# A four-layer cross-attention network: the first layer's attention tail with GpSimd and VectorE in written order

## The chip, the cores and the metric

The kernel runs on one core of a Trainium2 chip. The metric is the time of one execution on the device in microseconds (us). Three runs of the kernel before gave 1819.81, 1826.41 and 1832.21 us; the median is 1826.41. A core has five engines that run beside each other, each working through its own list of instructions in order: TensorE (PE in the profile; its weight loads are listed apart as PEld), VectorE (DVE), ScalarE (ACT), GpSimd (POOL) and SyncE (SP, which here only issues transfers). They wait for each other through semaphores.

## What is computed

Four layers in a row update 2048 tokens of width 256. Each layer adds a cross-attention to a context of 1601 rows and then a feed-forward part:

```python
x = x + _L0_xattn_ref(_layernorm(x, axis=-1), ctx_1024, ...)
x = x + _L0_ffn_ref(_layernorm(x, axis=-1), L0_ffn_gate_w, L0_ffn_experts)
x = x + _L1_xattn_ref(_layernorm(x, axis=-1), ctx_1024, mask_BxSxS2_ik0, L1_xattn_Wq, L1_xattn_Wk, L1_xattn_Wv)
x = x + _L1_ffn_ref(_layernorm(x, axis=-1), L1_ffn_fast_b, L1_ffn_w_fc, L1_ffn_w_proj, L1_ffn_u, L1_ffn_v, L1_ffn_gate)
...
```

The part that matters here is `_L1_xattn_ref`, an attention with one head of width 256 in which keys whose mask is 0 get a score of -1e10, and `_L1_ffn_ref`, whose two weight matrices are rounded to -1, 0 and 1 times a scale of each row. Layers are counted from 0 in the reference, so what the change's short name calls the first layer is L1.

## The kernel before, in words

The tokens are kept on chip as 16 tiles of 128 rows (`self.x`), in four chunks of four tiles. `network` (L2154) runs the layers. Everything from L1 on lies in a conditional block (L2164), chosen by a number that `experts0` works out.

**How the order of the work is set.** The kernel is written in a framework that records the instructions in the order of the source and then schedules them: for each engine it chooses an order by priorities and by its own estimate of when operands are ready. `tc.manual_schedule(engines=...)` excepts the engines it names, which keep the order of the source until the surrounding `ExitStack` closes. `experts0` (L552), `ffn1` (L1387), `ffn2` (L1522) and `attention3_tail` (L1947) name all four computing engines (`IN_ORDER`, L18), `attention0` names TensorE alone (L441). `attention1_tail`, which the change touches, names none.

**`attention1_tail` (L1101).** Only the last 400 of 1601 keys (L29, `K0`, `NTAIL`) are open. They are worked on as four key tiles of 100. L1123 to L1147 transpose the three weight matrices (L225, copied by ScalarE at L234) and make keys and values (L1134, L1143). Then each chunk of tokens goes through two parts.

The generator `prepare(c)` (L1149) makes a chunk ready:

- `fetch` (L789) has GpSimd gather the rows that the experts of layer 0 owe to the four tiles (L794, an indirect transfer each), and VectorE adds them (L799).
- `norm_steps` (L144): VectorE takes the statistics of each tile (L151, L152), GpSimd makes 1/sqrt of the variance (`rstd`, L156 and L157), VectorE normalises (`xn`, L171), TensorE transposes (L185), ScalarE copies out of the accumulator bank (`xnT`, L189).
- TensorE projects to queries (L1158); ScalarE copies them (L1162), VectorE copies them again as bf16 (L1163).
- For each of the four tiles TensorE makes bf16 scores (L1169) and adds the mask (L1173), and VectorE takes their maximum (L1174). The four maxima are transposed to a row (L247) and cast to `shift` by VectorE (L248).

The loop (L1183) then makes the scores of chunk c (L1192), takes the shift off in the same accumulation (L1195), has ScalarE take exponentials (L1196), and for each tile sums the values (L1202) and has VectorE divide and add (L1209 and L1210). The value sums use accumulator banks with tag "a", of which there are two, and all of `self.pm()` (transposes, projections, maxima) uses banks with tag "m", also two (L92). Between these steps the source calls `step(nxt, ...)`, which takes the next chunk's `prepare` a step further, and `step(beside, 2)` (L1207).

**`beside`** is `ffn1_weights` (L1253), the preparation of the next part's weights, a generator as well. Its VectorE work in this stage: the mean absolute values of the rows of `w_fc` (L1280 to L1283, L1289), eight ternary groups (two instructions, L1222 and L1223, then the scaling of `u`, L1293), the low-rank part (L1312 to L1332), the same for `w_pr` (L1280 to L1283 and four pairs of L1222 and L1223), and at the end the first input of `ffn1` (`inputs(0)`, L1366). TensorE transposes the ternary matrices (L1232, L1245), ScalarE copies them (L1235, L1249). GpSimd clears two tiles (L1304 and L1321). SyncE loads `w_fc`, `w_pr` and small inputs at the start, and later the weights of the following layers into the same three buffers (`wraw`, L63), each as soon as its buffer is free.

After this stage `ffn1` (L1379) runs; its first matmul is at L1396.

Of the kernel before, what the change touches and what calls it, by code (L numbers as in the profile page):

```python
# [40 lines left out]
def drain(gen):  # L41
    if gen is not None:
        for _ in gen:
            pass
# [10 lines left out]
class Net:  # L55
# [1045 lines left out]
    def attention1_tail(self, pre, mask, raw, due, beside=None):  # L1101

        tc, nc = self.tc, self.nc
        with ExitStack() as s:
# [44 lines left out]
            def prepare(c, made):  # L1149
                self.fetch(rows, range(c * TPC, (c + 1) * TPC), *due)  # L1150
                xnT = self.norm(c)
                yield
                q = qp.tile([P, 2, CH], F32, name="q")
                qb = qp.tile([P, 2, CH], BF16, name="qb")
                for o in range(2):
                    ps = self.pm()
                    for kc in range(2):
                        nc.tensor.matmul(  # L1158
                            ps, lhsT=wT["Wq"][:, kc, o * P : (o + 1) * P], rhs=xnT[:, kc, :],
                            start=kc == 0, stop=kc == 1,  # L1160
                        )
                    nc.scalar.copy(q[:, o, :], ps)  # L1162
                    nc.vector.tensor_copy(qb[:, o, :], ps)  # L1163
                yield
                m = self.small.tile([P, TPC], F32, name="m")
                for i in range(TPC):
                    ps = self.pm()
                    for kc in range(2):
                        nc.tensor.matmul(  # L1169
                            ps[:, :NTAIL], lhsT=qb[:, kc, i * P : (i + 1) * P], rhs=kb[:, kc, :],  # L1170
                            start=kc == 0, stop=False,
                        )
                    nc.tensor.matmul(ps[:, :NTAIL], lhsT=one, rhs=away, start=False, stop=True)  # L1173
                    nc.vector.tensor_reduce(m[:, i : i + 1], ps[:, :NTAIL], AX.X, ALU.max)  # L1174
                    yield
                shift = shifts[c % 2]
                self.row_from_columns(lambda i: m[:, i : i + 1], shift[0:1])
                made.append((q, shift))

            made = []  # L1180
            drain(prepare(0, made))
            self.ready = 0
# [1047 lines left out]
```

## Time and profile before

| what | value |
|---|---|
| median of three runs | 1826.41 us (1819.81 to 1832.21) |
| profiled execution, its own time | 1826.28 us |
| its span, from the first to the last instruction | 1824.2 us |
| mean granted TensorE clock | 0.976 |
| TensorE busy | 1699.6 us (93%) |
| VectorE, ScalarE, GpSimd busy | 909.8, 728.5, 690.8 us |
| first TensorE instruction of the stage (L225) | 863.3 us |
| first TensorE instruction of `ffn1` (L1396) | 978.15 us |

Times in the profile count from the start of the span; 2.1 us of the execution lie outside it. "Busy" counts the time in which an engine runs an instruction. In the list of groups a row is one line of the kernel on one engine: the operation, its output and inputs, how often it ran, its busy time and the mean duration of one in ns, and then the engine's idle time before these instructions and what ended it. In the list of waits a row says who waited for whom, for how long in all, how often, and the longest. In the table by stretches each row is a stretch of the span, its length, and then the busy time of each engine with the number of instructions, the granted TensorE clock (1.00 is full speed), the busy share of the transfer engines and what they moved. In the timeline a row is one instruction or a run of equal ones: start, duration, engine, line, operation, and in brackets the idle time before it and what ended it. A TensorE instruction on 32-bit data shows as two records, except for transposes.

VectorE and GpSimd reach the stage before TensorE does: VectorE's first instruction in it (L1114) starts at 831.80, GpSimd's (L1130) at 831.88, while TensorE is still in the last products of `experts0` (L557) until 863. In the order before, VectorE's first normalisation (L171) waits 24.1 us for GpSimd's `rstd`, which stands behind the clearing at L1304, and that starts at 867.66.

### The profile page before, as it was taken

The numbers are of one execution on the slowest core, as the hardware profiler recorded it, in microseconds if no ns is written. First come the engines' busy times: TensorE is split into PE (matmuls) and PEld (weight loads), VectorE is DVE, ScalarE is ACT, GpSimd is POOL, SyncE is SP. The second block draws the span as 40 slices with busy tenths as digits, with TensorE's granted clock in tenths as the row PEclk, the third lists the DMA queues.
The fourth block names the chain that finished last, engine by engine and source line by source line (L and its number), as shares of the span: only waits on it lengthen the run. The fifth ranks groups of instructions, "written<-read, shape, count | busy, mean of one in ns | idle before, by whom it ended". The sixth has DMA issues, their size and how long they took to land.

```text
span 1824.2 us, 21267 instructions
## 1 busy us (share of the span) xinstructions
PE 1699.6 (93%) x8102; PEld 848.0 (46%) x8102; DVE 909.8 (50%) x1737; ACT 728.5 (40%) x963; POOL 690.8 (38%) x477
## 2 busy tenths in 40 slices
PE   6879999999999998999999999999988789999898
PEld 3323334333333334444457863664576622332687
DVE  4664565555664543662844643422045567786300
ACT  3554443453443442223234522111135456666222
POOL 2047886876887683002202730100026400211210
PEclk9889999999999998999999999999989889999999
DMA  8870000000000000454300010000000001010651
GB/s 271 280 229 1 1 1 1 1 1 1 1 1 1 1 0 12 163 220 173 111 13 1 1 32 1 1 1 0 0 1 1 13 13 21 17 22 13 221 184 39
DMA packets 52461, 94.11 MB, mean 52 GB/s; under 512 B 10093, under 2 KB 37374, under 8 KB 51454
## 3 DMA queue, kind: packets, MB, share of 16 engines
q1 hardware_dynamic: 49776, 88.92, 14.8%
q0 software_dynamic: 768, 2.10, 0.4%
q10 hardware_dynamic: 1806, 1.64, 0.3%
q8 instruction: 66, 1.08, 0.2%
q14 instruction: 45, 0.37, 0.1%
HBM read 69.30 MB, written 19.01 MB: 48 GB/s over the span
## 4 chain that ended last, share of the span: by engine, by line
PE 72%; DVE 12%; ACT 5%; DMA 4%; POOL 3%; issue 3%; SPq 0%; ACTq 0%; DVEq 0%; POOLq 0%
PE pa L472 8%; PE psc L460 6%; PE pa L557 6%; PE psc L1058 5%; PE pa L1078 5%; PE psc L1980 4%; DVE mp L385 4%; PE pa L2143 3%; PE psc L2132 3%; DVE ri L422 3%; PE pa L1449 2%; PE psc L458 2%; ACT p L1987 2%; PE pm L380 2%; PE pm L431 2%
## 5 line engine op out<-in xcount | busy, mean ns | idle before, releaser
L481 POOL TENSOR_TENSOR sp<-sp,p 128x1024 f32<-128x1024 f32 (+1 forms) x176 | 418.5, 2378 | 57.7 <-ACT p L465 47.0
L385 DVE TENSOR_REDUCE mp<-pm 128x1 f32<-128x512 f32 x384 | 242.8, 680 | 159.7 <-PE pm L380 159.0
L465 ACT ACTIVATE p<-psc 128x1024 f32<-128x1024 f32 (+1 forms) x208 | 212.9, 1024 | 260.5 <-PE psc L460 166.9
L460 PE MATMUL psc<-qT,kT 64*128 64x512 f32 (+1 forms) x832 | 221.6, 594 | 0.0
L472 PE MATMUL pa<-p,v 128*64 128x512 f32 (+1 forms) x832 | 202.3, 608 | 0.0
L1987 ACT ACTIVATE p<-psc 100x1024 f32<-100x1024 f32 x128 | 124.4, 1021 | 62.7 <-PE psc L1980 54.7
L1965 DVE TENSOR_REDUCE ms<-psc 128x2 bf16<-128x800 f32 x128 | 124.2, 988 | 46.0 <-PE psc L1961 43.4
L380 PE MATMUL pm<-kb,qb 64*128 64x512 bf16 x384 | 100.5, 389 | 27.5 <-DVE mp L385 26.0
L557 PE MATMUL pa<-w_e,xe 128*128 128x512 f32 x256 | 118.7, 614 | 0.0
L472 PEld LDWEIGHTS pa<-p,v 128*64 128x64 f32 (+1 forms) x832 | 50.9, 137 | 129.8 <-issue 126.8
L1058 PE MATMUL psc<-q,kT 128*128 128x512 f32 (+1 forms) x208 | 102.2, 610 | 0.0
L171 DVE TENSOR_SCALAR xn<-x,mv,rstd 128x256 f32<-128x256 f32 x128 | 58.2, 512 | 87.7 <-PE pm L185 52.2
L156 POOL TENSOR_SCALAR rstd<-mv 128x4 f32<-128x4 f32 x32 | 9.8, 308 | 228.6 <-DVE mv L152 185.2
L1078 PE MATMUL pa<-v,p 128*128 128x257 f32 (+1 forms) x416 | 95.3, 382 | 0.0
L460 PEld LDWEIGHTS psc<-qT,kT 64*128 64x128 f32 (+1 forms) x832 | 86.0, 185 | 19.5 <-issue 6.3
L1980 PE MATMUL psc<-q,kT 32*100 32x512 f32 x512 | 82.0, 653 | 13.2 <-ACT p L1987 11.5
L458 PE MATMUL psc<-sh,negz 64*128 64x512 bf16 (+1 forms) x416 | 87.7, 384 | 2.1 <-ACT sh L407 2.0
L1030 DVE TENSOR_REDUCE mp<-pm 128x1 f32<-128x512 f32 x64 | 34.4, 571 | 102.5 <-PE pm L1025 102.2
L1078 PEld LDWEIGHTS pa<-v,p 128*128 128x128 f32 (+1 forms) x416 | 77.5, 190 | 11.8 <-issue 0.2
L567 ACT COPY y<-pa 128x512 f32<-128x512 f32 x64 | 37.6, 587 | 96.6 <-PE pa L557 94.3
L557 PEld LDWEIGHTS pa<-w_e,xe 128*128 128x128 f32 x256 | 48.0, 194 | 55.6 <-issue 52.3
L479 POOL TENSOR_TENSOR sp<-p,p 128x1024 f32<-128x1024 f32 x16 | 37.7, 2354 | 89.4 <-ACT p L465 89.4
(376 smaller groups left out, 2730.2 us busy)
## 6 DMA issues: line engine op xcount, KB each, us to landing
table<-y SPq DMA_DIRECT2D x32, 512.0 KB, 3.2
w<-in_L_ffn_w_dram SPq DMA_DIRECT2D x16, 1024.0 KB, 6.2
head<-in_mask_BxSxS_ik_dram SPq DMA_DIRECT2D x16, 600.5 KB, 4.0
head<-in_mask_1x1xSxS_ik_dram SPq DMA_DIRECT2D x16, 600.5 KB, 4.0
bc<-turned SPq DMA_DIRECT2D x7, 1024.0 KB, 7.0
tail<-in_mask_BxSxS_ik_dram SPq DMA_DIRECT2D x16, 200.0 KB, 4.1
tail<-in_mask_1x1xSxS_ik_dram SPq DMA_DIRECT2D x16, 200.0 KB, 3.6
x<-in_x_dram SPq DMA_DIRECT2D x16, 128.0 KB, 4.0
```

Source lines behind the costliest of these rows:

```text
L380: nc.tensor.matmul(pair[j][:, :wd], lhsT=qb[h, i * P : (i + 1) * P], rhs=kb[h, hp, k0 : k0 + wd], start=True, stop=True,)
L385: nc.vector.tensor_reduce(mp[:, i, j, n : n + 1], pair[j][:, :wd], AX.X, ALU.max)
L460: nc.tensor.matmul(sc[:r, j, :], lhsT=kT[h, hp, kt * P : kt * P + r], rhs=q[h, :], start=False, stop=True,)
L465: nc.scalar.activation(p[:r], sc[:r], AF.Exp, scale=DH**-0.5)
L472: nc.tensor.matmul(acc[h, :], lhsT=v[:r, kt, hp * P + h.start : hp * P + h.stop], rhs=p[:r, j, :], start=kt == 0, stop=kt == NKT - 1,)
L481: nc.gpsimd.tensor_tensor(sums[:r], sums[:r], p[:r], ALU.add)
L557: nc.tensor.matmul(ps, lhsT=xnT[t // TPC][:, kc, (t % TPC) * P : (t % TPC + 1) * P], rhs=ew[kc][:, 2 * h : 2 * h + 2, :], start=kc == 0, s ...
L1058: nc.tensor.matmul(sc[:r, j, :], lhsT=kT[:, kc, ks], rhs=q[:, kc, :], start=kc == 0, stop=False)
L1078: nc.tensor.matmul(acc[:, : D + 1], lhsT=p[:r, kt, i * P : (i + 1) * P], rhs=v[:r, kt, :], start=kt == 0, stop=kt == NKT - 1,)
L1965: nc.vector.tensor_reduce(ms[u % 2][:, i, 64 * k + DH : 64 * k + 64 : 32], ps[:, :, :NTAIL], AX.X, ALU.max)
L1980: nc.tensor.matmul(sc[j // 2][:TR, j % 2, :], lhsT=kT[h, g, kt * TR : (kt + 1) * TR], rhs=q[u][h, :], start=True, stop=True,)
L1987: nc.scalar.activation(p[:TR], sc[k][:TR], AF.Exp, scale=DH**-0.5)
```

## The change

One line is added in `attention1_tail`, ahead of the first chunk's `prepare`:

```diff
@@ -1177,6 +1177,7 @@
                 self.row_from_columns(lambda i: m[:, i : i + 1], shift[0:1])
                 made.append((q, shift))
 
+            s.enter_context(tc.manual_schedule(engines={mybir.EngineType.Pool, mybir.EngineType.DVE}))
             made = []
             drain(prepare(0, made))
             self.ready = 0
```

From there to the end of the function GpSimd and VectorE keep the order of the source; that takes in the steps of `prepare` and of `beside` that are called from it. TensorE and ScalarE are scheduled as before, around the two fixed lists, and their order differs too. No instruction is added or taken away. The order in which SyncE issues its transfers is the same. Lines after L1179 have a number higher by one in the changed kernel.

What the changed lists look like: on GpSimd the row fetches of chunk 1 come after the `rstd` of chunk 0, those of chunk 2 after that of chunk 1, and those of chunk 3 after that of chunk 2 and after both clearings (L1304, L1321), where before twelve fetches stood ahead of the first `rstd`. VectorE's list, with the lines of before, goes:

```
chunk 0: L799 x4, (L151 L152) x4, L171 x4, L1163 x2, L1174 x4, L248
chunk 1: L799 x4, (L151 L152) x4, L171 x4, L1163 x2, L1174 x3
w_fc:    L1280 to L1289, (L1222 L1223 L1293) x4
         L1209 L1210, L1174, (L1222 L1223 L1293) x4, L1209 L1210, L248, (L1209 L1210) x2
chunk 2: L799 x4, (L151 L152) x4, L171 x4, L1163 x2, L1174 x3
         L1312 x2, L1209 L1210, L1174, L1314 to L1332, L1209 L1210, L248
w_pr:    L1280 to L1283, (L1222 L1223) x4, (L1209 L1210) x2
chunk 3: L799 x4, (L151 L152) x4, L171 x4, L1163 x2, L1174 x3
         L1209 L1210, L1174, then the statistics of ffn1's first inputs
...
```

## The prediction

> **What bounds the kernel now.** I read the page first, for the busiest engine and the chain of work that ended last:
>
> ```profile
> span 1824.2 us, 21267 instructions
> PE 1699.6 (93%) x8102; PEld 848.0 (46%) x8102; DVE 909.8 (50%) x1737; ACT 728.5 (40%) x963; POOL 690.8 (38%) x477
> ...
> PE 72%; DVE 12%; ACT 5%; DMA 4%; POOL 3%; issue 3%; SPq 0%; ACTq 0%; DVEq 0%; POOLq 0%
> ```
>
> TensorE carries the chain, so a wait costs time only where TensorE stands still for it. Next the busy time by stretch, for the stage that the change touches: its TensorE work runs from 863.3 us (the first L225) to 978.15 us (the first L1396 of ffn1).
>
> ```profile
> core 0: us, PE busy (x) PEld busy (x) DVE busy (x) ACT busy (x) POOL busy (x), PEclk, DMA share, GB/s
> 863.30:978.15 114.85, 112.31 (x438) 58.99 (x436) 66.09 (x183) 35.34 (x58) 13.20 (x18) 1.00 0.17 54
> 863.30:886.96 23.66, 21.12 (x82) 10.52 (x80) 15.02 (x43) 8.42 (x20) 7.93 (x10) 1.00 0.58 182
> 886.96:908.00 21.04, 21.04 (x89) 11.59 (x89) 19.21 (x54) 5.50 (x9) 1.48 (x2) 1.00 0.16 51
> 908.00:936.00 28.00, 28.00 (x108) 13.57 (x107) 17.20 (x51) 10.30 (x15) 2.53 (x4) 1.00 0.09 29
> 936.00:960.00 24.00, 24.00 (x98) 12.85 (x97) 8.93 (x25) 6.74 (x11) 1.26 (x2) 1.00 0.00 1
> 960.00:978.15 18.15, 18.15 (x67) 10.46 (x65) 5.72 (x14) 4.38 (x6) 0.00 (x0) 1.00 0.00 0
> ```
>
> TensorE idles 114.85 - 112.31 = 2.5 us, all before 886.96. That caps any gain. VectorE is nearly full from 887 to 908 (19.21 of 21.04) yet holds nobody up. The waits of TensorE in the stage, and GpSimd's longest in front of work:
>
> ```profile
> PE pm L1169 <- DVE qb L1163: 0.9, 2, 0.5
> PE pm L225 <- ACT WkT L234: 0.8, 1, 0.8
> PE psc L1195 <- DVE shift L248: 0.3, 1, 0.3
> ...
> POOL b L1304 <- PE pm L1134: 19.7, 1, 19.7
> ```
>
> **The change, part by part.** No instruction is added or removed; order alone changes. VectorE now runs the layer strictly as written: a chunk's row additions, its statistics, its normalisation, its maxima, and the weight preparation (`beside`) in one lump where each step is called. GpSimd likewise. TensorE and ScalarE are still scheduled, and their order is new too. I laid the new orders side by side with durations from this trace. VectorE's lumps:
>
> ```profile
> L1280 DVE TENSOR_REDUCE sc<-w_fc 128x8 f32<-128x2048 f32 x1 | 2.3, 2289 | 0.0
> L1222 DVE TENSOR_SCALAR lo<-w_fc,nhalf 128x256 bf16<-128x256 f32 x8 | 2.7, 339 | 0.0
> L1223 DVE SCALAR_TENSOR_TENSOR tfc<-w_fc,half,lo 128x256 bf16<-128x256 f32 x8 | 3.8, 472 | 0.0
> ...
> L1280 DVE TENSOR_REDUCE sc<-w_pr 128x2 f32<-128x2048 f32 x1 | 2.2, 2240 | 0.0
> L1222 DVE TENSOR_SCALAR lo<-w_pr,nhalf 128x512 bf16<-128x512 f32 x4 | 1.9, 472 | 0.0
> L1223 DVE SCALAR_TENSOR_TENSOR tpr<-w_pr,half,lo 128x512 bf16<-128x512 f32 x4 | 3.0, 738 | 0.0
> ```
>
> In the timeline a dependent VectorE instruction starts about 0.05 us after its producer's end, an independent one about 0.08 before. So one w_fc group (L1222, L1223, then L1293) takes 0.93 us and one w_pr pair 1.32. On TensorE, start to start, a score instruction L1192 takes 0.945 us (two records), L1195 0.34, a value instruction L1202 0.485, a tile's maxima (L1169 twice, L1173) 0.61. The line numbers are those of before. PSUM tag "a" has two buffers: the third L1202 group of a chunk needs the first freed by L1210, the fourth the second.
>
> *1, hand-over from chunk 0.* Removed: the 0.9 and 0.3 us above (score instructions now stand in front of the waiting L1169). Added: shift 0.8 (0.11 hand-over, 0.67 cast, 0.05), because chunk 1's transposes no longer stand there. Then VectorE, from the shift on: 0.6, four row additions 1.56, four statistics pairs 2.2, GpSimd's rstd 1.5 (L156 and L157 with hand-overs), first xn 0.45: 6.3 us; TensorE: 0.6 of the wait, four L1192 and four L1195 (5.1): 5.7. It waits 0.5, and 0.2 for the next xn. Net +0.3.
>
> *2, w_fc lump.* It sits between the third maximum of chunk 1 and L1210 of chunk 0's first tile. VectorE from the third maximum's matmul: 0.6 for the maximum, L1280 2.2, L1281 to L1289 0.6, four groups 3.75, L1209 and L1210 0.7: 7.9 us. TensorE meanwhile: one L1202 0.5, the last maxima 0.6, three L247 0.3, four L1192 3.8: 5.2. Wait 2.7. Then the L1232 transposes: one of the two "m" banks is held for the shift, whose cast waits behind the second half of the lump, so twice they wait for ScalarE's copy (0.11 + 0.59 + 0.05), and once 0.9 for the last ternary group. In all 2.7 + 2.4 = +5.1.
>
> *3, chunk 2's rows.* As in 1, VectorE needs 0.7 (L1209, L1210) and 5.7 (additions to first xn); TensorE has 6.0 us of filler. Wait 0.5 and 0.2: +0.7.
>
> *4, w_pr lump.* First 0.5 for L1210 behind L1314 to L1332. Then shift 0.6, L1280 2.2, small ones 0.6, four pairs 5.3, L1209 and L1210 0.6: 9.3 us, against 1.9 + 5.1 + 0.5 (L1202, scores, L1245) = 7.6 on TensorE. Wait 1.6. Together +2.1.
>
> *5, chunk 3's rows.* VectorE: L1209 and L1210 0.6, then 5.8 to the first xn: 6.4. TensorE has only eight L1202, 3.9: wait 2.4. Then L1158 waits for the copy of xnT without filler, 0.7. +3.1.
>
> *6, ffn1's statistics.* Eight pairs (3.4 us), spread over idle VectorE time before, now stand ahead of an L1210: 0.5 + 3.4 + 0.8 = 4.7 against 2.8 of TensorE work. +1.9.
>
> Sum: 0.3 + 5.1 + 0.7 + 2.1 + 3.1 + 1.9 = 13.2 us.
>
> *Clock.* Here is what a light stretch does elsewhere in this trace, in three neighbouring stretches and the transposes in the middle one:
>
> ```profile
> 1407.98:1411.40 3.42, 2.41 (x18) 2.15 (x18) 3.42 (x13) 2.88 (x3) 2.15 (x2) 1.00 0.00 0
> 1411.40:1414.81 3.41, 1.39 (x8) 1.00 (x9) 3.41 (x3) 0.47 (x1) 2.04 (x1) 0.98 0.00 0
> 1414.81:1418.22 3.41, 3.41 (x10) 2.67 (x9) 3.09 (x12) 0.70 (x3) 0.00 (x0) 0.52 0.00 0
> ...
> 1413.65 1.09 PE L185 MATMUL pm<-ident,xn 128*128 128x128 f32 x6 [2.02 <-DVE xn L171]
> ```
>
> TensorE busy 1.39 of 3.41 us was followed by 3.4 us at half clock: 1.7 us lost. Gaps 2 and 5 can each make such a stretch, depending on where the stretches fall: 0 to 3.4; I take one, +1.7. The Trainium skill, "TensorE: Matmul & The Clock Gate", section "HAM oscillation — how this bites in real kernels", warns only of idle gaps over about 3.4 us. By that rule gaps of 2.7 and 2.4 are free and the sum stays 13.2 (1839.5); the row above, halved after a gap of 2.02, contradicts it.
>
> *Moved on queues, costed at nothing.* GpSimd's two memsets (L1304, L1321) and the fetches of rows 12 to 15 move behind chunk 2's rstd, from about 868 to 922; first use about 940 and 951, the fetch lands within 6.1 us. Fetches 8 to 11 wait for chunk 1's rstd (889), used at 916. On SP the load of w_dn waits for the last w_fc group (891 to about 912), the next layer's three weights for the last w_pr pair (910 to about 951); first uses are 1064 and 1057.8. If such a cover were gone, the lateness would be paid whole. Chunk 0's rstd leaves its place behind L1304: its xn is ready about 25 us sooner, but TensorE did not wait for it.
>
> Total 13.2 + 1.7 = 14.9 us. After the stage ffn1 is again bound by TensorE, so nothing returns it. The profiled execution took 1826.28 us, the median is 1826.41: 1826.3 + 14.9 = 1841 us.
>
> **The rivals.** *A. The new TensorE order covers VectorE's lumps.* For: at hand-overs 1 and 3 it does, to 0.7 us. Against: both lumps outlast the filler by 1.6 to 2.7. If only 1 stood: 1826.6 us. *B. GpSimd freed from L1304 gains.* For: 19.7 us of wait vanish. Against: the cap, 2.5 us: 1823.8. *C. The half clock follows every gap, and it is slower by over 1%.* Places: 2 (twice), 4, 5, 6. With four at 1.7 it is 13.2 + 6.8: 1846.3. It decides from three on (18.3 us). For: the rows above. Against: gaps of 1.6 and 1.9 leave TensorE over 1.5 busy in 3.4, more than 1.39, and at 2.41 the clock stayed 1.00.
>
> **How the numbers follow.** Forecast 0.55 (its own range 1836 to 1844), A and its shades 0.10, B 0.04, C or lumps dearer than summed 0.31. About 1% (18.3 us) is what a measurement of this kernel can tell from no change; the forecast, A and most of B lie within it. Faster 0.02, same 0.67, slower 0.31. The range goes down to 1832 (half of the waits gone) and up to 1852 (20 us of C, and 6 us, since the runs of before spread by as much above the median).
>
> **What would show it.** Right: TensorE idle near 16 us between the first L225 and ffn1, in waits of L1202 for L1210 and of L185 for L171, the longest about 2.7 us, beside the lumps; a slice at half clock at one of them; the rest of the span unchanged. Wrong: no idle time beside the lumps (A), half clock three times or more (C), or a wait for a row fetch or a memset, whose cover I would have misjudged.

## The result, and the profile after

The changed kernel took 1849.54 us in the median (1842.94 to 1855.18), the kernel before 1828.36 beside it: ratio 1.0113 [1.0085, 1.0141]. Taken a second time (e5 below) it was 1848.57 against 1826.42, 1.0120 [1.0091, 1.0150]. That is 21 to 22 us slower, inside the range given (1832 to 1852), above the forecast of 1841 and its own range (1836 to 1844). The prediction gave 0.67 to a change of up to about 1% and 0.31 to a larger loss; the measured ratio lies a little past 1%, but its interval holds 1% too, so it does not decide between the two.

The page of the changed kernel (profiled execution 1852.77 us), first its span and busy times, then the shares of the chain of work that ended last:

```profile
span 1850.8 us, 21249 instructions
PE 1716.3 (93%) x8090; PEld 857.5 (46%) x8102; DVE 917.8 (50%) x1737; ACT 727.7 (39%) x963; POOL 689.7 (37%) x477
...
PE 71%; DVE 14%; ACT 5%; DMA 4%; POOL 3%; issue 3%; SPq 1%; ACTq 0%; DVEq 0%; POOLq 0%
```

TensorE still carries the chain, but VectorE has 14% of it in place of 12, and TensorE's own busy time grew by 16.7 us though it executes the same instructions. Where that happened shows in the busy time by stretch of the changed kernel; the first row is the stage from its first L225 to the first L225 of the next layer, the others stretches within it (columns as in the prediction; the lines of the changed kernel behind L1179 are one higher):

```profile
864.90:1081.00 216.10, 199.53 (x887) 130.07 (x886) 118.90 (x275) 77.84 (x118) 65.42 (x58) 0.95 0.10 31
...
908.00:936.00 28.00, 22.47 (x77) 12.90 (x76) 16.39 (x48) 6.54 (x10) 6.38 (x8) 0.82 0.18 56
936.00:960.00 24.00, 22.17 (x82) 10.29 (x82) 18.40 (x39) 8.33 (x10) 0.00 (x0) 0.97 0.06 18
960.00:978.15 18.15, 16.72 (x64) 8.75 (x63) 8.60 (x25) 3.79 (x7) 1.28 (x2) 0.95 0.08 20
978.15:1000.00 21.85, 20.10 (x69) 11.52 (x68) 10.66 (x35) 4.38 (x6) 2.52 (x4) 0.84 0.00 1
```

In the kernel before the same stage ran from 863.3 to 1057.8, all at full clock:

```profile
863.30:1057.80 194.50, 188.57 (x886) 125.25 (x885) 113.42 (x274) 77.80 (x118) 63.08 (x56) 1.00 0.10 32
```

That is 194.5 us, of which TensorE was busy 188.57. So the stage has grown by 21.6 us, and that splits in two: idle time 5.93 -> 16.57, +10.6, and busy time 188.57 -> 199.53, +11.0. The rest of the 26.6 us by which the profiled span grew (1.6 us ahead of the stage, 3.4 behind it) lies in stages that the change does not touch. Those vary by some us from profile to profile: two profiles of the changed kernel have 769.9 and 767.0 us behind the stage, while the stage itself took 216.1 and 216.0. The waits of TensorE in the changed kernel's stage (total, times, longest):

```profile
PE pa L1203 <- DVE x L1211: 4.8, 3, 2.8
PE pm L185 <- DVE xn L171: 2.7, 3, 1.3
PE pa L1203 <- DVE ri L1210: 1.5, 1, 1.5
PE pm L1233 <- DVE shift L248: 0.8, 1, 0.8
...
PE psc L1196 <- DVE shift L248: 0.8, 1, 0.8
PE pm L1233 <- ACT wfT L1236: 0.7, 1, 0.7
```

These are the waits of the prediction's steps: the value matmuls (L1202 before) wait for the division that stands behind a weight lump, the transposes wait for the normalised rows, and the waits for qb (L1169 before) are gone. What the waits do to the clock shows in the changed kernel's busy time by stretches of 3.41 us (in each trace the half-clock stretches all begin on one grid of this length, and the stretches are cut along it), a light one and its successor each time:

```profile
907.30:910.70 3.40, 0.76 (x2) 0.00 (x0) 3.26 (x13) 0.00 (x0) 0.00 (x0) 1.00 0.00 0
910.70:914.10 3.40, 3.29 (x8) 2.64 (x9) 3.29 (x11) 0.00 (x0) 0.00 (x0) 0.50 0.00 0
...
955.00:958.45 3.45, 1.96 (x11) 0.79 (x10) 3.27 (x8) 1.99 (x3) 0.00 (x0) 1.00 0.01 2
958.45:961.85 3.40, 3.40 (x10) 2.67 (x9) 3.30 (x12) 0.00 (x0) 0.00 (x0) 0.50 0.81 230
...
978.95:982.35 3.40, 1.67 (x10) 1.23 (x8) 3.08 (x14) 0.00 (x0) 1.69 (x4) 1.00 0.00 0
982.35:985.80 3.45, 3.45 (x10) 1.74 (x9) 1.47 (x5) 0.00 (x0) 0.84 (x1) 0.50 0.02 5
```

TensorE is busy 0.76, 1.96 and 1.67 us of 3.4, and what follows runs at half clock for 10.2, 3.4 and 6.8 us: six stretches, 20.5 us, where the kernel before had none. Half of six full stretches is 10.2 us, which is nearly all of the 11.0 by which the busy time grew.

### The profile page after: what moved, and what is told of

It reads as the page before. It is cut to its first block, busy times and chain, and to the rows that moved or that the text cites. A ratio compares the mean times of both kernels' runs of the same rounds, so it can differ in the third digit from the quotient of the medians.

```text
span 1850.8 us, 21249 instructions
## 1 busy us (share of the span) xinstructions
PE 1716.3 (93%) x8090; PEld 857.5 (46%) x8102; DVE 917.8 (50%) x1737; ACT 727.7 (39%) x963; POOL 689.7 (37%) x477
## 3 DMA queue, kind: packets, MB, share of 16 engines
q10 hardware_dynamic: 1806, 1.64, 0.3%
## 4 chain that ended last, share of the span: by engine, by line
PE 71%; DVE 14%; ACT 5%; DMA 4%; POOL 3%; issue 3%; SPq 1%; ACTq 0%; DVEq 0%; POOLq 0%
PE pa L472 8%; PE psc L460 6%; PE pa L557 6%; PE psc L1058 5%; PE pa L1078 5%; PE psc L1981 4%; DVE mp L385 4%; PE psc L2133 3%; PE pa L2144 3%; DVE ri L422 3%; PE pa L1450 2%; PE psc L458 2%; PE pm L380 2%; PE pa L1998 2%; PE pm L431 2%
## 5 line engine op out<-in xcount | busy, mean ns | idle before, releaser
L1981 PE MATMUL psc<-q,kT 32*100 32x512 f32 x512 | 83.0, 659 | 13.2 <-ACT p L1988 11.5
```

Source lines behind the costliest of these rows:

```text
L1981: nc.tensor.matmul(sc[j // 2][:TR, j % 2, :], lhsT=kT[h, g, kt * TR : (kt + 1) * TR], rhs=q[u][h, :], start=True, stop=True,)
```

## The experiments

Theory V: VectorE's work, put in lumps by the source's order, makes TensorE wait, and the waits make the half clock; each is about half of the loss. Rivals: G, it is GpSimd's order; O, it is the fixed order as such or TensorE's new order, whatever VectorE has to do; L, the half clock in this stage is luck of the moment. The measure throughout is the stage, from its first L225 to the next layer's, in the profiled execution; beside it the ratio of the whole time to the kernel before, measured beside it each time (its medians were 1826.4 to 1833.6 us).

| kernel | stage us | TensorE idle | busy | half-clock stretches | ratio |
|---|---|---|---|---|---|
| before | 194.5 | 5.9 | 188.6 | 0 | |
| changed | 216.1 | 16.6 | 199.5 | 6 | 1.0113 [1.0085, 1.0141] |
| e5, changed again | 216.0 | 16.6 | 199.4 | 6 | 1.0120 [1.0091, 1.0150] |
| e1, GpSimd alone | 202.9 | 12.2 | 190.7 | 1 | 1.0050 [1.0034, 1.0066] |
| e2, VectorE alone | 219.8 | 20.0 | 199.8 | 6 | 1.0137 [1.0113, 1.0161] |
| e3, casts, scheduled | 201.6 | 10.9 | 190.7 | 2 | 1.0046 [1.0030, 1.0062] |
| e4, casts, in order | 209.3 | 14.1 | 195.2 | 4 | 1.0063 [1.0039, 1.0087] |
| e6, division first | 208.8 | 15.1 | 193.7 | 2 | 1.0091 [1.0070, 1.0112] |
| e7, gaps filled | 212.2 | 9.8 | 202.4 | 2 | 1.0086 [1.0066, 1.0106] |
| e10, rows ahead | 211.1 | 14.9 | 196.2 | 5 | 1.0071 [1.0052, 1.0090] |

**e1, GpSimd alone in order; e2, VectorE alone.**

```diff
-s.enter_context(tc.manual_schedule(engines={Pool, DVE}))
+s.enter_context(tc.manual_schedule(engines={Pool}))      # e1
+s.enter_context(tc.manual_schedule(engines={DVE}))       # e2
```

> Only GpSimd is kept in the source's order; VectorE is scheduled as before. Measure: TensorE's time from the stage's first L225 to the next layer's first L225, 194.5 us in the kernel before and 216.1 in the changed one; PE waits of the stage about 2.5 and 12 us. Theory V (VectorE's lumps make the waits, and the waits make the half-clock stretches): the lumps are gone, so 194 to 196 us, no wait of a value matmul for its division and no half-clock stretch in the stage; whole time 1824 to 1830. Rival G (GpSimd's order carries the loss, its rstd or its fetches coming late): 205 us or more, with waits of L185 behind it. Rival L (the half clock in the stage is luck of the phase, not of the waits): half-clock stretches here as well, 10 us of them, without waits.

> Only VectorE is kept in the source's order; GpSimd is scheduled as before. Theory V: as slow as the changed kernel, 212 to 219 us from the stage's first L225 to the next layer's (before 194.5, changed 216.1), the same waits of L1203 (2 to 3 us at each weight lump), perhaps with a longer wait for the normalised rows of chunk 1 (2.1 us in place of 0.6), since GpSimd's rstd stands behind the memset that waits for its memory. Whole time 1842 to 1852. Rival G: 195 to 200 us, near the kernel before.

e2 came as theory V has it: 219.8 us, the same waits of L1203 (2.75, 0.33, 1.49, 1.73), and longer ones for xn (3.13 and 2.47), six half-clock stretches. VectorE's order is enough for the whole loss. e1 missed: expected 194 to 196, it took 202.9 and the whole kernel 0.5% longer. The cause shows in its timeline (start, length, engine, line, in brackets the idle time before and its releaser), for VectorE, GpSimd and TensorE:

```profile
873.64 2.29 DVE L1281 TENSOR_REDUCE sc<-w_fc 128x8 f32<-128x2048 f32 x1 [30.40 <-PE pm L1143]
...
876.11 0.23 POOL L156 TENSOR_SCALAR rstd<-mv 128x4 f32<-128x4 f32 x1 [37.14 <-DVE mv L152]
...
878.06 2.31 PE L185 MATMUL pm<-ident,xn 128*128 128x128 f32 x8 [3.72 <-DVE xn L171]
```

VectorE, scheduled anew since GpSimd's order had changed, has the reduction of w_fc in front of the last aggregate of chunk 0's statistics (L152, 875.85). The reduction does not start until 873.64; the releaser named does not touch w_fc, and in e3 ScalarE's first cast of w_fc waited for that weight's load until 872.84, so the load is the likely cause. Behind it hang GpSimd's rstd, and, in order behind that, the fetches of chunk 1 (877.7 to 882.7; in the kernel before they had been issued by 843). TensorE waits 3.72 for xn and 2.38 more for qb. In the changed kernel, with VectorE in order too, that rstd runs at 844.93. So GpSimd's order alone does cost, 8.4 us of the stage, but by a mechanism that the two together do not have.

**e3, e4, the ternary instructions taken off VectorE.** The same edit to the kernel before (e3) and the changed one (e4):

```diff
-            self.ternary(tp, tfc[:, o, :], wfc[:, o, :], half[:, o : o + 1], nhalf[:, o : o + 1])
+            nc.scalar.copy(tfc[:, o, :], wfc[:, o, :])
...
-            self.ternary(tp, tpr[:, o, :], wpr[:, o, :], half[:, o : o + 1], nhalf[:, o : o + 1])
+            nc.scalar.copy(tpr[:, o, :], wpr[:, o, :])
```

> The kernel before, with the ternary weights of ffn1 left out: in place of the two VectorE instructions of each piece ScalarE casts the weight to bf16 (so the weights used are not the ternary ones). It is the base for the next kernel. Theory V and its rivals alike: 194 to 198 us from the stage's first L225 to the next layer's, since VectorE's lumps were off the path before; waits of TensorE 3 to 5 us.

> The changed kernel with the same edit: ternary instructions left out, ScalarE casts instead (so the weights used are not the ternary ones). The in-order engines stay in order; only the two big lumps on VectorE shrink, by 4 x 0.8 us each half of w_fc and 4.8 us for w_pr. Theory V: the waits at the lumps vanish, the change then costs 1 to 5 us beside the scheduled kernel with the same edit, in place of 21.6: 196 to 201 us from the stage's first L225 to the next layer's, one wait of 1.5 to 2 us left (at ffn1's statistics), 0 to 3.4 us at half clock. Rival O (the order as such costs, that is TensorE's own new order, or the rows' additions and statistics at the hand-overs): 10 us or more remain. Rival L (half clock by luck): the waits go, but 10 us of half-clock loss stay.

Both stages are longer than expected by a wait that the edit itself made in both: L1143 stands 4.6 us behind ScalarE, whose first cast waits for the load of w_fc, and two half-clock stretches follow. Between the two, the order costs 7.7 us in place of 21.6: idle +3.2, busy +4.5, two half-clock stretches more. The whole times, 1839.76 against 1838.10, differ by less: in these two profiles the parts outside the stage took 5.4 us less in e4, so the 7.7 rests on the stage alone. The waits at both lumps are gone, as theory V says; left are 1.25 for the rows of chunk 2 and 1.73 at ffn1's statistics, each followed by half clock. The sum of 1 to 5 us was too low, again by the clock. Rival O (10 us or more) is not borne out, but about a third of the loss stays without the ternary lumps.

**e5, e6, e7: the same waits again, the wait moved, the wait filled.**

```diff
                     step(nxt, 1)
-                    step(beside, 2)
                     ri = self.small.tile([P, 1], F32, name="ri1")
                     nc.vector.reciprocal(ri, acc[:, D : D + 1])
                     nc.vector.scalar_tensor_tensor(x, acc[:, :D], ri, x, ALU.mult, ALU.add)
+                    step(beside, 2)
```

is e6; e7 adds to the changed kernel, ahead of tile 2 of chunks 0 and 2, and once more behind the first scores of chunk 2:

```diff
+                    for n in {(0, 2): (2, 2), (2, 2): (2, 2)}.get((c, i), ()):
+                        fill = self.pm()
+                        for _ in range(n):
+                            nc.tensor.matmul(fill, lhsT=self.ident, rhs=q[:, 0, :], start=True, stop=True)
                     acc = self.pa()
```

> The changed kernel itself once more, as the base for the next two on the same chip. Theory V (VectorE's lumps make TensorE wait about 12 us in the stage, and the waits make the half-clock stretches): 214 to 220 us from the stage's first L225 to the next layer's, half-clock stretches again near the waits of L1203, 17 to 21 us of them; whole time 1845 to 1853. Rival L (the half clock in the stage was luck): the waits again, but the half-clock stretches elsewhere or gone, 203 to 208 us.

> The changed kernel with a tile's division and update (L1210, L1211) written ahead of the weight preparation's step instead of behind it. Theory V: the three waits of L1203 for x and ri (2.75, 1.48, 1.74 us) vanish, since what TensorE waited for no longer stands behind a lump; the lump now delays the next chunk's maxima, shift and rows instead, so that part returns as waits of L185 for xn (up to 3.7 us) and of L247 for m (1.3). 3 to 7 us less than the changed kernel from the stage's first L225 to the next layer's: 209 to 213. Rival O (the lumps delay in whatever place): no change beyond 2 us.

> The changed kernel with eleven matmuls that nothing uses (128x512 f32, 0.47 us each, 5.2 us in all) put on TensorE ahead of the three waits of L1203 that were 2.75, 1.48 and 1.74 us long: four, three and four of them. The work waited for is the same, so it comes no sooner. If a wait cost only its own length, the time stays as it is (5.0 us of the added work lies in the waits, 0.2 outside). Theory V with the clock as second cost: the stretches of 3.41 us around these three waits stay busy above 2 us, so that the half clock behind them goes: three to five of six half-clock stretches, 1.7 us each, so 5 to 9 us less than the changed kernel, 207 to 212 us from the stage's first L225 to the next layer's, though TensorE has more to do. Rival L (half clock by luck): as slow as the changed kernel or 5 us slower.

e5: the six half-clock stretches lie in the same places, 10.2, 3.4 and 6.8 us, behind the same waits. Rival L, as chance from run to run, falls here. But the stage also began at the same place of the 3.41 us grid in both profiles (2.0 and 2.1 us into a stretch), so e5 does not show what another place would do; e2 does (see e8). e6: the waits of L1203 are gone, and what was expected in their place is there, in this line of its timeline:

```profile
954.66 1.74 PE L185 MATMUL pm<-ident,xn 128*128 128x128 f32 x8 [3.64 <-DVE xn L171]
```

Idle time fell by only 1.5 us; busy time fell by 5.8, since two half-clock stretches are left of six. 208.8 us, where 209 to 213 were expected.

e7 is the clearest. Its eleven matmuls are 22 records that start 0.43 us apart; from the first record of each group to the next instruction they take 9.7 us in all, nearly twice what the expectation's text says. The stage by stretch, and TensorE's wait of L1203 (L1211 in this kernel):

```profile
861.30:1073.50 212.20, 202.44 (x909) 130.78 (x908) 118.95 (x275) 77.87 (x118) 65.52 (x58) 0.98 0.10 32
```

```profile
PE pa L1211 <- DVE x L1219: 0.3, 1, 0.3
```

TensorE has 9.7 us more to do, waits 6.8 less, and has two half-clock stretches in place of six, which is worth 6.8: 9.7 - 6.8 - 6.8 = -3.9 us, and -3.9 is what the stage shows. That is less than the 5 to 9 us expected, since more work was added than planned. The whole kernel took 1842.50 against 1848.57 in the median of six runs each (1839.28 to 1844.61 and 1839.37 to 1855.20). A wait's length and its clock are separate costs, and the second can be taken away while the first stays.

**e8, gaps of graded length, in the kernel before.** In ffn1, ahead of every second slot:

```diff
+            def gap(size):
+                first = self.pm(BF16)
+                tc.nc.tensor.transpose(first[:, :P], self.identb, self.identb)
+                tc.nc.vector.tensor_copy(slow[:, :P], first[:, :P])
+                w = wfT.rearrange("p k f -> p (k f)")[:, :size].bitcast(F32)
+                tc.nc.vector.tensor_tensor(slow[:, :size], w, w, ALU.add)
+                then = self.pm(BF16)
+                tc.nc.tensor.transpose(then[:, :P], slow[:, :P], self.identb)
```

> The kernel before, with seven gaps of graded length put into ffn1, where TensorE is busy without a break: a transpose, a VectorE sum over 256 to 2048 columns behind it, and a transpose that needs the sum. Gaps of about 0.8, 1.1, 1.3, 1.6, 2.0, 2.4 and 2.7 us, 8 us apart or more. It measures what a gap costs beyond its own length. By the reading behind the prediction (half clock once TensorE is busy 1.4 us or less in a stretch of 3.41): only the gaps of 2.0 and more that fall within one stretch, so one to three half-clock stretches. By the changed kernel's trace (half clock also behind stretches with 1.68 and 1.93 us): gaps from 1.6 us up, two to four. Rival L (no relation): half clock behind short gaps as often as behind long ones.

Other VectorE work stood ahead of the gaps' sums, so the gaps came out at 6.37, 1.64, 5.63, 1.96, 5.90, 2.17 and 5.54 us. The whole took 1868.85 us in its one run, the stage 232.5 in place of 194.5: 29.2 of gaps, and nine half-clock stretches. The four over 5 us are each followed by two. The three short ones tell more; here those of 1.64 and 1.96 with the stretch behind them:

```profile
1005.06:1008.48 3.42, 1.78 (x17) 1.61 (x16) 2.60 (x4) 1.42 (x3) 1.89 (x1) 1.00 0.00 0
1008.48:1011.89 3.41, 3.41 (x21) 2.95 (x21) 2.93 (x9) 1.50 (x3) 1.28 (x2) 1.00 0.00 0
...
1035.78:1039.19 3.41, 1.45 (x14) 1.27 (x12) 2.58 (x4) 1.34 (x3) 1.89 (x1) 0.97 0.01 2
1039.19:1042.61 3.42, 3.42 (x10) 2.71 (x10) 3.42 (x16) 0.35 (x1) 0.42 (x1) 0.53 0.00 0
```

The gap of 1.96 lies in one stretch, leaves 1.45 busy, and the next runs at half clock; the gap of 1.64 (1.78 busy) does not do it; the longer gap of 2.17 falls across two stretches (2.46 and 2.20 busy) and does not either. So a gap's place in the grid counts as well as its length. e2 shows the same in the stage itself. There the wait of 2.75 us at the w_fc lump ends at 910.34 and falls across two stretches:

```profile
906.12:909.53 3.41, 1.48 (x4) 0.33 (x2) 3.27 (x13) 0.00 (x0) 0.00 (x0) 1.00 0.00 0
909.53:912.95 3.42, 2.31 (x13) 1.88 (x14) 3.28 (x12) 0.13 (x1) 0.00 (x0) 1.00 0.00 0
```

Full clock goes on behind both, and half clock follows only behind the next waits, from 916.4; in the changed kernel the same wait left one stretch with 0.76 busy, and half clock followed at once.

**e9, the same filling where the kernel before has half clock; e10, the source rearranged.** e9 adds unused bf16 matmuls to the kernel before in three waits outside the stage. e10 is the changed kernel with e6's edit, a yield after every ternary group of w_fc, and each chunk's rows, statistics and normalisation stepped among the value matmuls two chunks earlier:

```diff
+            self.fill(bank, kb[:, 0, :CH], 18)          # e9, one of the three places
             for n in range(5):
                 step(done, 1)
+                self.fill(bank, kb[:, 0, :CH], 2 if n < 4 else 0)
```

```diff
+                then = head(c + 2) if c + 2 < NCH else None     # e10: fetch, statistics, xn
...
+                    step(then, 2)
                     step(beside, 2)
```

> The kernel before, with matmuls that nothing uses (128x512 bf16, about 0.23 us) put into TensorE's waits at three places outside the changed stage, each followed by half clock in the kernel before: layer 0's first maxima (73 to 96 us; 20.5 us of half clock from 80.1), layer 0's last sums (693 to 705 us, a wait of 4.84; 10.2 us from 697.9) and layer 3's first maxima (1448 to 1461 us, a wait of 2.96; 23.9 us from 1452.2). Nothing is taken out and what is waited for comes no sooner. If the clock follows the light stretches, as the filled gaps of the changed stage showed: these 54.6 us of half clock shrink to under 25, and the part of them in which TensorE was the limit comes back: 2.5 us, 3.9 us and 5 to 7 us, so 1812 to 1819 us, faster than both kernels. Rival: if the half clock there has another cause, the added matmuls are time spent and nothing returns: 1826 to 1832.

> The changed kernel (GpSimd and VectorE still in the source's order), with the source rearranged: a tile's division ahead of the weights' step, a yield after every ternary group of w_fc in place of every second, and a chunk's rows, statistics and normalisation written among the value matmuls of the chunk two before instead of in one piece at the hand-over. Theory V: what costs is where the source puts VectorE's work, so the waits shrink from 12 to about 8 us, none much over 2 us (the waits for xn down to 1.0, the rest at the two lumps), and with them the half-clock stretches, to three or fewer: 202 to 208 us from the stage's first L225 to the next layer's (before 194.5, changed 216), whole time 1835 to 1841. Rival O (an engine in a fixed order costs, wherever the source puts the work): 212 us or more.

e9 missed: 1834.13 against 1833.57, 1.0003 [0.9989, 1.0017]. The half clock at the three places did shrink, from 54.6 us to 17 (behind the first of them, from 107 to 136 us, it grew from 6.8 to 17, and over the whole span it fell only from 26 stretches to 22), but no time came back. At layer 3's first maxima the stretch from its first maximum to its first score stayed 10.7 us (10.8 with the filling): there TensorE waits for VectorE at either clock. Ahead of it the filling stood in the way: 4.9 us in place of 3.2 from the last ffn2 matmul to the first maximum. So half clock cost nothing here, where TensorE was not the limit behind the light stretch, as it is in the changed stage; the other two places were not taken apart. This was no version that beats both kernels.

e10 missed its 202 to 208 us: 211.1, five half-clock stretches, waits no fewer but in other places: 2.50 for the maxima (L247 for m) and 1.95 for the shift, both behind ternary groups and other VectorE work between 905 and 914. At 0.9 us below rival O's 212, with nearly as much idle time as the changed kernel, it does not speak against O; e4 does.

## Why the prediction was right or wrong

Which way the time moved, and by which waits, was right; of the sum, the waits were 2.5 us too high and the clock 9.3 us too low, so that the stage lost 21.6 us where 14.9 were forecast. By its own steps, the sum of waits first, from the changed kernel's timeline:

- *1, hand-over:* 0.77 for the shift and 0.57 for xn stand against 1.2 removed, +0.1 (predicted +0.3). Right.
- *2, w_fc lump:* 2.75 at L1203 (predicted 2.7), 0.80 and 0.67 at the transposes (predicted 2.4 together): +4.2 against 5.1.
- *3, chunk 2's rows:* 1.31 against 0.7.
- *4, w_pr lump:* 0.34 and 1.48 against 0.5 and 1.6.
- *5, chunk 3's rows:* 0.81 and 0.62 against 2.4 and 0.7. In e2, where VectorE is in order as well, the first was 2.47; in the changed kernel TensorE's half clock from 958.5 gave VectorE time to catch up (3.4 us at half clock is 1.7 us less work done, and 2.4 - 1.7 = 0.7), which is argued from where the two lie, not tested.
- *6, ffn1's statistics:* 1.74 against 1.9.
- *Sum:* 10.7 us against 13.2, the same as the 10.6 by which idle time grew. No wait for a row fetch or a memset appeared: the moves on queues cost nothing, as said.
- *Clock:* predicted +1.7 with bounds 0 and 3.4, measured about 11 (six stretches). This term failed: 9.3 us too little, against 2.5 too much in the waits. The working took one row (1.39 busy, then half clock) for the limit, and held gaps of 1.6 and 1.9 to be safe because they leave over 1.5. The changed kernel's stretches with 1.96 and 1.67 busy were followed by half clock, and a light stretch that is followed by another wait (1.93 busy at half clock, 914.1 to 917.5) holds the half clock on. Nor does a stretch at half clock have to be light for another to follow: those from 910.7 and 982.4, shown above, were busy for 3.29 of 3.40 and all of 3.45 us, and the next was at half clock too; why is not shown. The trace of before had shown as much: its stretch at 735 was busy 2.61 and the next ran at half clock.
- *Rivals:* A did not happen: both lumps outlasted the filler. B's gain is not there, and e1 shows GpSimd alone losing. C, given 0.31 with slower by over 1%, is what happened at its places 2, 4 and 6, and not at 5. Its condition (three stretches or more) was met twice over; its sum, 13.2 + 6.8, was near because waits too high and clock too low offset each other.
- *What would show it:* idle time near 16 us up to ffn1 was too high (about 13: the stage's 16.6 less the 3.4 that the kernel before idles behind ffn1's first matmul), the longest wait of 2.7 us beside a lump was right, and "half clock three times or more" was the sign named for C.

## What to carry to other kernels

Putting an engine with slack into the source's order turns its spare work into lumps where the source steps it; count, for each lump, what the bounding engine has left to do before it needs that engine's next result. Price a wait of TensorE twice, by its length and by the half clock that may follow, and read the second from all such places of the trace, not from one; where TensorE is the limit behind the wait, each stretch of 3.41 us at half clock costs about 1.7 us more. Fixing one engine's order makes the scheduler order the others anew, so a change to one alone can cost by a path that the change to both does not have.

## What the runs showed of the hardware that was not expected

- Work that nothing uses made the kernel faster: 9.7 us more for TensorE, 3.9 us less in the stage and 6.1 us less in the median (e7).
- All half-clock times here are multiples of 3.41 us (but for the one at the end of a trace), and in each of the twelve traces they start on one grid of that length, with the span beginning 0.2 to 2.1 us into one of its steps. The Trainium skill, "TensorE: Matmul & The Clock Gate", section "Part 1: The HAM clock gate (the "warmup" mystery)", has a window of that length that runs free of the kernel, which agrees with these lengths and with e8 and e2, where the place of a gap in the grid mattered.
- The same page's rule to have no idle gaps over about 3.4 us (section "HAM oscillation — how this bites in real kernels") is not enough here: 1.96 us within one stretch was followed by half clock (e8), as were 2.75, 1.48 and 1.74 in the changed kernel.
- What stays open is the limit. By the profile's busy time, 1.96 and 1.93 were followed by half clock, and 1.78 (e8) and 1.48 (e2) were not; in the kernel before, the stretch ahead of the half clock at 820.8 was fully busy. Busy time alone does not decide it. The traces hint at what the instructions are: 2.8 us of that fully busy stretch are matmuls with only 8 moving columns (L715), and so is most of the one at 735 (L594); in e4 a stretch busy 2.05 (from 921.45), 1.49 of it transposes, was followed by half clock, while the one of e2 with 1.48 holds no transpose. No run tested this.
